# Token groups of 128 instead of 112 behind the attention of a two-layer image model

## The chip, the cores and the metric

The kernel runs on one core of a Trainium2 chip. The core has a matrix engine (TensorE, PE in the profile, with its weight loads as PEld), three engines for elementwise work (VectorE, DVE; ScalarE, ACT; GpSimd, POOL), a queue engine (SyncE, SP), an on-chip memory SBUF of 128 partitions, a small accumulator memory PSUM, and 16 DMA engines. The metric is the time of one execution on the device in microseconds (us). Before the change it is 1744.01 us, the median of 3 runs (1739.07 to 1748.02).

## The reference

The input x is a float32 image batch, 2 x 256 channels x 56 x 56. Two layers follow; a token is one pixel with its 256 channels, and there are N = 6272 of them.

```
x = x + proj_o(attention_7x7(LN_channels(x)))            # layer 0, 8 heads
t = tokens(x)
t = t + (LN_t(t) + sum over the 2 best of 8 experts: w_e * MLP_e(LN_t(t)))
x = image(t)
x = x + relu(o1 + bn(tri_conv(o1)))                       # layer 1
    with o1 = relu(bn(tri_conv(LN_channels(x))))
t = tokens(x)
t = t + sum over the 2 best of 8 experts: p_e * MLP_e(LN_t(t))
x = image(t)
```

The hidden size of an expert is 256 in layer 0 and 512 in layer 1. tri_conv is a 3 x 3 convolution with weights quantised to -1, 0, 1; bn takes its statistics over the whole batch.

## The kernel before

An image is cut into 7 strips of 8 rows, 14 strips in all, 448 tokens each (`NT`). A strip is cut into 4 groups (`NTT`) of 112 tokens (`TT`), each a block of 8 rows by 14 columns: a group is what stands on the partitions at one time. There are 56 groups (`NTOK`).

The attention has its own use for the block of 112 queries, which the change leaves alone: queries, keys, scores and weighted sums (L1441 to L1540) run per block, and the loop over blocks is a hand-written order on every engine. What comes behind it, once a strip is complete, is `leave` (L1545): the normalised result is copied into `oc` (DVE, L1589), per group four records of `pw` on PE (two channel halves, L1602) project it, and DVE adds the input `xr` (L1610). Then the strip is handed to the routing.

Both layers route alike. `norm` (L765) takes per group the mean and variance (`bn_stats`, L713, `bn_aggr`, L715, both DVE), scales (`u`, ACT, L735), transposes on PE (`pu`, L781) with a copy on ACT (`ut`, L786), and multiplies with the gate (`pl`, L795): per group two matmuls, four records, that stream 8 columns each. In layer 0 the sum of token and norm is stored in the DRAM buffer `x_mid`. `settle` (L809) takes the two best experts on DVE, and ranks the tokens of each expert by small matmuls with triangular and all-one matrices (`rk`, L854 to L857). From the ranks come row numbers `pos`, and POOL sends each group's rows by two indirect DMAs into the expert buffer `xs` (L891), in layer 1 with three small operations ahead of them (L887 to L889). A strip in layer 0 is settled with its neighbour, in layer 1 as the list `BATCHES` says.

The experts (`experts_in_order`) read `xs` in tiles of 256 rows: transposes `pt` (L1112), first product `ph` (L1144), second product `py` (L1163), and an indirect DMA that scatters the result to `ys` in token order (L1175). The first tiles of a layer can start when the first 10 (layer 0) or 9 (layer 1) strips are routed (`FIRST`); the rest of the rows is sent beside the running experts.

Between the layers, `combine` (L1786) runs per strip: it fetches the two results of each token (`got`, L1211), adds them with their weights (DVE, L1230, and ACT, L1222), normalises over the channels, transposes (`pu`, L1239), and two copies on ACT write the strip into the padded image `pad` (L1801). The first three strips are done before the first convolution, the others beside it, driven by the convolution's step counter. The convolution works by units of two strips and four components (order 1, 2, 0, 3): `component` (L1818 to L1820) forms differences `v` of rows of `pad` on POOL, and splits them in `hi` (ACT) and `lo` (DVE) for the matmuls `pc` (L1845). Component 3 of a unit reads one row beyond the unit, which is the first row of the next strip. The second convolution (L1988) works on the image alone. `residual` (L2118) adds it up in channel layout (DVE, L2127; ACT, `nr`, L2130), transposes back to tokens (`pt`, L2139), and adds `x_mid` (L2145); `all_strips` (L2167) interleaves residual, norm and settle of consecutive strips in an order written out by hand, and `fence` (L2156) waits for the early scatters on POOL before the experts of layer 1 start.

The last loop (L2268) fetches `got` (L2273, two groups a piece), adds with weights (DVE, L2278), transposes (L2287), copies into the strip's `o_out` (ACT, L2293), and stores a whole strip (L2298).

Of the kernel before, what the change touches and what calls it, by code (L numbers as in the profile page):

```python
# [11 lines left out]
F32 = mybir.dt.float32  # L12
# [9 lines left out]
P = 128  # L22
# [46 lines left out]
EARLY = tuple(max(0, (TOP * NT * n - E * (G - 1)) // G) for n in FIRST)  # L69
# [563 lines left out]
def metaformer(ctx: ExitStack, tc: tile.TileContext, a: dict, out: bass.AP, flag):  # L633
# [31 lines left out]
    ids = rt.tile([TT, NTOK], F32, tag="ids", name="ids")  # L665
# [4 lines left out]
    x_mid = dram.tile([len(STRIPS), TT, NTT, C], F32, tag="x_mid", name="x_mid", bufs=1)  # L670
# [7 lines left out]
    minus_half = const.tile([TT, NTT], F32, tag="minus_half", name="minus_half")  # L678
# [11 lines left out]
    order = const.tile([TT, E], F32, tag="order", name="order")  # L690
# [3 lines left out]
    before_f = const.tile([TT, TT], F32, tag="before_f", name="before_f")  # L694
    nc.sync.dma_start(before_f, a["before"])
    before_w = const.tile([TT, TT], BF16, tag="before_w", name="before_w")
    nc.vector.tensor_copy(before_w, before_f)
    all_w = const.tile([TT, P], BF16, tag="all_w", name="all_w")
# [3 lines left out]
    base_t = tabs[:TT, T_BASE : T_BASE + E]  # L702
# [5 lines left out]
    def token_stats(tp, src, eps, root):  # L708

        stats = tp.tile([TT, NTT, 6], F32, tag="t_stats", name="t_stats")  # L710
        mv = tp.tile([TT, NTT, 2], F32, tag="t_mv", name="t_mv", bufs=3)
        for t in range(NTT):
            nc.vector.bn_stats(stats[:, t, :], src[:, t, :])  # L713
        for t in range(NTT):
            nc.vector.bn_aggr(mv[:, t, :], stats[:, t, :])  # L715
        rstd = tp.tile([TT, NTT], F32, tag="t_rstd", name="t_rstd", bufs=3)
        nmr = tp.tile([TT, NTT], F32, tag="t_nmr", name="t_nmr", bufs=3)
        nc.vector.tensor_scalar_mul(nmr, mv[:, :, 0], -1.0)
        if root:
            nc.scalar.activation(rstd, mv[:, :, 1], AF.Sqrt, bias=eps[:TT])  # L720
        yield
        if root:
            nc.vector.reciprocal(rstd, rstd)
            nc.vector.tensor_tensor(nmr, nmr, rstd, ALU.mult)
        else:
            nc.gpsimd.tensor_tensor(rstd, mv[:, :, 1], eps[:TT].to_broadcast([TT, NTT]), ALU.add)
            nc.gpsimd.tensor_tensor(rstd, rstd, minus_half, ALU.pow)
            nc.gpsimd.tensor_tensor(nmr, nmr, rstd, ALU.mult)
            yield
            yield  # L730
        return rstd, nmr

    def scaled(dest, src, rstd, nmr):
        for t in range(NTT):
# [10 lines left out]
    def routing(layer, wp, tp, ps):  # L745
# [4 lines left out]
        if layer == 1:  # L750
            gate_b = wp.tile([TT, E], F32, tag="gate_b", name="gate_b")
            nc.sync.dma_start(gate_b, a[pre + "gate_b"].partition_broadcast(TT))
        lgs = wp.tile([TT, NTOK, E], F32, tag="lgs", name="lgs")
        most = wp.tile([TT, TOP, NTOK], F32, tag="most", name="most")
        pos = wp.tile([TT, TOP, NTOK], I32, tag="pos", name="pos")
        wgt = rt.tile([TT, TOP, NTOK], F32, tag="wgt", name="wgt", bufs=2)
        chosen = wp.tile([TT, NTOK], F32, tag="chosen", name="chosen")
        seen = wp.tile([TT, E], F32, tag="seen", name="seen")
        nc.vector.memset(seen, 0.0)
        seen_b4 = wp.tile([TT, E], BF16, tag="seen_b4", name="seen_b4")  # L760
# [4 lines left out]
        def norm(i, src, late=False):  # L765
# [4 lines left out]
            row = rows[i] = tp.tile([TT, NTT, RW], F32, tag="u", name="u", bufs=U_BUFS[layer])  # L770
            u = row[:, :, :C]
            if layer == 0 or i >= FIRST[1]:
                eng.memset(row[:, :, R_EX + 1 :], 0.0)
                eng.tensor_copy(row[:, :, R_ID], ids[:, i * NTT : (i + 1) * NTT])
            scaled(u, src, rstd, nmr)
            yield
            ut = tp.tile([P, KC, NT], F32, tag="ut", name="ut", bufs=1)
            for k in range(KC):
                pu = ps.tile([P, 512], F32, tag="aux", name="pu")
                for t in range(NTT):  # L780
                    nc.tensor.transpose(  # L781
                        pu[:, t * TT : (t + 1) * TT],
                        u[:, t, k * P : (k + 1) * P],
                        ident[:TT, :TT],
                    )
                nc.scalar.copy(ut[:, k, :], pu[:, :NT])  # L786
            if layer == 0:
                eng.tensor_tensor(src, src, u, ALU.add)
                nc.sync.dma_start(x_mid[i], src)
                yield  # L790
            lg = lgs[:, i * NTT : (i + 1) * NTT, :]
            pl = ps.tile([TT, NTT, E], F32, tag="pl" if layer else "aux", name="pl")
            for t in range(NTT):
                for k in range(KC):
                    nc.tensor.matmul(  # L795
                        pl[:, t, :],
                        ut[:, k, t * TT : (t + 1) * TT],
# [4 lines left out]
            if layer == 1:  # L802
                yield
                nc.vector.tensor_tensor(lg, pl, bcast(gate_b, 1, [TT, NTT, E]), ALU.add)
# [4 lines left out]
        def settle(strips):  # L809


            n = len(strips) * NTT
            t0 = strips[0] * NTT
            us = [rows.pop(i) for i in strips]
            full, row = [TT, n, E], (TT, n)

            def small(name, shape=(TT, n, E), dt=F32):
                return tp.tile(list(shape), dt, tag=f"{name}_{n}", name=name, bufs=1)
# [13 lines left out]
            hot = small("hot", (TT, TOP, n, E))  # L832
            at = [chosen[:, t0 : t0 + n], small("at", (TT, n))]
            rest = small("rest")
            first_max(lg, m[0], hot[:, 0], at[0])
            for q, u in enumerate(us if layer == 0 or strips[0] >= FIRST[1] else ()):
                small_eng.tensor_copy(u[:, :, R_EX], at[0][:, q * NTT : (q + 1) * NTT])
# [7 lines left out]
            seen_b = small("seen_b", (TT, E), BF16)  # L845
            nc.vector.tensor_copy(seen_b, seen)
            here = small("here", (TT, E))
# [5 lines left out]
            rk = ps.tile([TT, n, E], F32, tag="aux", name="rk")  # L853
            nc.tensor.matmul(rk, before_w, hots, start=True, stop=False)  # L854
            nc.tensor.matmul(rk, all_w[:, :TT], bcast(seen_b, 1, full), start=False, stop=n == 1)
            for t in range(n - 1):
                nc.tensor.matmul(  # L857
                    rk[:, t + 1 :, :],
                    all_w[:, :TT],
# [1555 lines left out]
```

## Time and profile before

| what | value |
|---|---|
| median of 3 runs | 1744.01 us (1739.07 to 1748.02) |
| profiled execution, own time | 1758.43 us |
| its span in the profile | 1756.6 us |
| mean granted TensorE clock | 0.901 |

The prediction shows the lines of the profile that it rests on. Two ways of reading recur. A line of a group of instructions names the source line, the engine, output <- input with their shapes, the count, busy time and the mean of one in ns, and the engine's idle time just before with what ended it. A line of a window gives start and end, length, then the busy microseconds and instruction count of each engine in that stretch, the granted clock, the share of time that the DMA engines were busy, and GB/s. A float32 matmul appears as two records. Matmuls are pipelined: where some stand in a row, the time of the row minus the last one, divided by the others, is the pitch at which they follow each other, and it is shorter than the duration of one.

Where the time lies, by the starts of the first instructions of each stage:

| stage | us of the span |
|---|---|
| attention, with routing of layer 0 beside it | 0 to 512 |
| experts of layer 0 | 512 to 808 |
| first strips back into the image | 808 to 840 |
| first convolution, other strips beside it | 840 to 1005 |
| second convolution | 1005 to 1150 |
| residual, norm and routing of layer 1 | 1150 to 1295 |
| experts of layer 1 | 1295 to 1690 |
| last additions and output | 1690 to 1756.6 |

### The profile page before, as it was taken

The page shows a single profiled execution, that of the slowest core. Times are in us where ns is not written, and L with a number is a line of the kernel's source. Part 1 is how long each engine was busy: PE and PEld are TensorE (multiplying, and loading weights), DVE is VectorE, ACT ScalarE, POOL GpSimd, SP SyncE. Part 2 cuts the span into 40 slices and gives each one's busy share as a digit, 9 for nine tenths or more (in the row PEclk, how much of TensorE's full clock was granted, in tenths as well). Part 3 has the DMA queues.
Part 4 walks back from the last instruction along what each step waited for, and adds up shares of the span by engine and source line. Part 5 has one row for each costly group of instructions (what it writes and reads, how often), then busy time and mean ns, then how long its engine had stood idle before and what let it go on. Part 6 is the DMA issues. An engine that isn't in the chain of part 4 may idle for free. (4 is left out here: it accounts for less than half of the span.)

```text
span 1756.6 us, 26034 instructions
## 1 busy us (share of the span) xinstructions
PE 1514.2 (86%) x8613; PEld 1185.1 (67%) x8613; DVE 973.3 (55%) x2697; ACT 700.4 (40%) x1386; POOL 672.9 (38%) x772
## 2 busy tenths in 40 slices
PE   5999998999868968994799969957689999999964
PEld 3555565555547757783688768746578888888842
DVE  4456676456645417794899888778733111111147
ACT  2544343353333324454454363235433334333322
POOL 2112345253343565453143323327835552222210
PEclk9999999899979989997899989955579999999975
DMA  7122324221166768795754000014467768888869
GB/s 237 43 65 87 107 86 124 70 81 60 55 192 195 246 220 320 255 336 160 198 151 123 3 0 1 11 47 128 134 215 266 266 228 303 286 278 294 287 182 306
DMA packets 93679, 291.78 MB, mean 166 GB/s; under 512 B 20711, under 2 KB 36027, under 8 KB 83776
## 3 DMA queue, kind: packets, MB, share of 16 engines
q1 hardware_dynamic: 68528, 231.79, 41.9%
q0 software_dynamic: 21200, 51.82, 8.2%
q10 hardware_dynamic: 3808, 6.42, 1.0%
q8 instruction: 70, 1.15, 0.3%
q14 instruction: 73, 0.60, 0.1%
HBM read 218.51 MB, written 74.20 MB: 167 GB/s over the span
## 5 line engine op out<-in xcount | busy, mean ns | idle before, releaser
L1144 PE MATMUL ph<-ut,w 128*128 128x256 f32 (+1 forms) x1472 | 311.5, 362 | 10.3 <-DMA w<-in_L_experts 5.3
L1173 DVE TENSOR_TENSOR y<-py,w 128x512 f32<-128x512 f32 (+1 forms) x120 | 76.8, 640 | 419.0 <-PE py L1163 349.6
L1163 PE MATMUL py<-w,h 128*128 128x256 f32 x1288 | 300.6, 382 | 3.5 <-DVE y L1173 1.5
L1144 PEld LDWEIGHTS ph<-ut,w 128*128 128x128 f32 x1472 | 251.6, 195 | 39.8 <-DMA w<-in_L_experts 6.0
L1163 PEld LDWEIGHTS py<-w,h 128*128 128x128 f32 x1288 | 245.0, 192 | 38.1 <-DVE y L1173 1.9
L891 POOL DMA_INDIRECT xs<-u,pos x224 | 218.3, 974 | 116.1 <-issue 52.8
L1175 POOL DMA_INDIRECT ys<-y,dest x136 | 137.4, 1010 | 242.0 <-DVE dest L1119 107.5
L1151 ACT ACTIVATE h<-ph,w 128x256 f32<-128x256 f32 (+1 forms) x368 | 162.6, 448 | 118.3 <-PE ph L1144 93.5
L1520 ACT ACTIVATE ex<-sc 112x476 f32<-112x476 f32 (+3 forms) x224 | 117.3, 573 | 178.2 <-PE sc L1510 162.5
L1116 ACT COPY ut<-pt 128x512 f32<-128x512 f32 (+1 forms) x120 | 65.1, 543 | 268.4 <-PE pt L1112 214.4
L1845 PE MATMUL pc<-lo,wq 128*128 128x448 f32 x336 | 131.5, 393 | 7.0 <-DVE lo L1820 6.9
L1845 PE MATMUL pc<-hi,wq 128*128 128x448 f32 x336 | 130.9, 392 | 3.4 <-DVE x L1869 3.2
L1540 DVE TENSOR_TENSOR acc<-av,acc 128x238 f32<-128x238 f32 (+3 forms) x224 | 87.5, 407 | 76.3 <-PE av L1530 65.6
L1530 PE MATMUL av<-ex,vals 112*64 112x238 f32 (+3 forms) x896 | 124.6, 399 | 5.8 <-DVE acc L1540 5.5
L1175 POOL DMA_INDIRECT ys<-y,to x81 | 81.8, 1009 | 119.7 <-DVE dest L1119 65.1
L1988 PE MATMUL pc<-hi,wq 128*128 128x448 f32 (+1 forms) x288 | 102.8, 366 | 17.9 <-ACT hi L1955 9.4
L1501 PE MATMUL sc<-q_im,keys 32*112 32x238 f32 (+3 forms) x896 | 98.6, 427 | 7.0 <-ACT ex L1520 6.8
L1988 PE MATMUL pc<-lo,wq 128*128 128x448 f32 (+1 forms) x288 | 101.8, 363 | 0.2 <-DVE lo L1956 0.2
L1818 POOL TENSOR_TENSOR v<-pad 128x928 f32<-128x928 f32 (+1 forms) x28 | 56.2, 2017 | 100.4 <-DVE lo L1820 49.5
L1530 PEld LDWEIGHTS av<-ex,vals 112*64 112x64 f32 x896 | 56.4, 141 | 55.8 <-issue 27.2
L1112 PE MATMUL pt<-ident,xg 128*128 128x128 f32 x434 | 71.2, 285 | 25.1 <-DMA xg<-xs 11.8
L1112 PEld LDWEIGHTS pt<-ident,xg 128*128 128x128 f32 x434 | 56.5, 148 | 39.8 <-ACT ut L1116 14.4
(279 smaller groups left out, 2532.3 us busy)
## 6 DMA issues: line engine op xcount, KB each, us to landing
w<-in_L_experts SPq DMA_DIRECT2D x64, 1154.0 KB
w<-in_L_experts SPq DMA_DIRECT2D x56, 641.0 KB
xg<-xs SPq DMA_DIRECT2D x97, 260.0 KB
acc<-in_fresh SPq DMA_DIRECT2D x14, 896.0 KB
got<-ys SPq DMA_DIRECT2D x14, 896.0 KB
got<-ys SPq DMA_DIRECT2D x28, 448.0 KB
xt<-in_x_tok SPq DMA_DIRECT2D x14, 448.0 KB
xr<-in_x_tok SPq DMA_DIRECT2D x14, 448.0 KB
```

What stands on the lines that cost most here:

```text
L891: w = nc.gpsimd.indirect_dma_start(xs[:, :], bass.IndirectOffsetOnAxis(ap=pos[:, j, t0 + t : t0 + t + 1], axis=0), us[t // NTT][:, t % NTT ...
L1112: nc.tensor.transpose(pt[:, k, i * P : (i + 1) * P], d["xg"][:, i, k * P : (k + 1) * P], ident)
L1144: nc.tensor.matmul(ph[:, :g], w1[:, k, f * P : (f + 1) * P], d["ut"][:, k, :g], start=k == 0, stop=k == KC - 1,)
L1151: nc.scalar.activation(d["h"][:, f, :g], ph[:, :g], AF.Gelu, bias=b1[:, f : f + 1])
L1163: nc.tensor.matmul(py[:, i, :], d["h"][:, f, i * P : (i + 1) * P], w2[:, f, :], start=f == 0, stop=f == NF - 1,)
L1175: o = nc.gpsimd.indirect_dma_start(ys[:, :], bass.IndirectOffsetOnAxis(ap=d["to"][:, i : i + 1], axis=0), y[:, i, :], None, bounds_check=T ...
L1501: nc.tensor.matmul(sc[h // 2][:, h % 2, :nq], keys[g][p, c, tx * TT : (tx + 1) * TT], q_im[p, c, r0:r1, c0:c1], start=True, stop=False,)
L1520: nc.scalar.activation(e[:, :, :nq], sc[j][:, :, :nq], AF.Exp, scale=HD**-0.5)
L1530: nc.tensor.matmul(av[VW * i : VW * (i + 1), :nq], vals[g % 3][:, tx, 2 * c + j, 2 * i : 2 * i + 2, :].rearrange("p a d -> p (a d)"), ex[j ...
L1540: added = nc.vector.tensor_tensor(d, av[:, :nq].rearrange("p (h w) -> p h w", w=c1 - c0), d, ALU.add)
L1845: nc.tensor.matmul(pc[:, :NT], wq[:, k, c, dx * C + o * P : dx * C + (o + 1) * P], part[:, :, k, dx : dx + W], start=m == 0, stop=m == 2 * ...
L1988: nc.tensor.matmul(pc[:, : 2 * ns * W], wq[:, k, c, dx * C + o * P : dx * C + (o + 1) * P], part[:, : 2 * ns, k, dx : dx + W], start=m == ...
```

## The change

Two neighbouring strips hold 896 tokens, seven groups of 128. Behind the attention the even strip of a pair now has three groups and the odd strip four; there are 49 groups (`NGR`). The block is 8 rows by 8 columns, two blocks a group. An even strip has seven blocks, so its last one is left over: it becomes half of the first group of the odd strip, together with the odd strip's own last block. A group can thus be made only of tokens that lie in two strips, and the buffers from which groups are read become rings of 512 columns, in which the even strip fills columns 64 to 511 and the odd strip 0 to 447.

```diff
+BW = 8
+NGR = N // P
+RING = NT + P // 2
+def groups_of(i):
+
+    at = 2 * NT // P * (i // 2) + NT // P * (i % 2)
+    return at, NT // P + i % 2
...
-    x_mid = dram.tile([len(STRIPS), TT, NTT, C], F32, tag="x_mid", name="x_mid", bufs=1)
+    x_mid = dram.tile([N, C], F32, tag="x_mid", name="x_mid", bufs=1)
...
-        for t in range(NTT):
+        for t in range(n):
             nc.vector.bn_stats(stats[:, t, :], src[:, t, :])
...
-            for t in range(NTT):
+            for t in range(ng):
                 for k in range(KC):
                     nc.tensor.matmul(
                         pl[:, t, :],
-                        ut[:, k, t * TT : (t + 1) * TT],
+                        ut[:, k, t * P : (t + 1) * P],
                         gate[:, k, :],
```

The image is written by runs of neighbouring blocks. An even strip writes one run of six blocks (48 of its 56 columns); an odd strip writes three: its own last block, the last block of the even strip, and its six others. So an even strip stands complete in the image only once the odd one has been written.

```diff
+    def runs_of(i, at=0, n=None):
+
+        ng = groups_of(i)[1]
+        runs = []
+        for t in range(at, ng if n is None else at + n):
+            col = (t - at) * P
+            if i % 2 and not t:
+                runs += [(col, i, NB - 1, 1), (col + P // 2, i - 1, NB - 1, 1)]
+                continue
+            x = 2 * (t - i % 2)
+            if runs and runs[-1][1] == i and runs[-1][2] + runs[-1][3] == x:
+                runs[-1] = (*runs[-1][:3], runs[-1][3] + 2)
+            else:
+                runs.append((col, i, x, 2))
+        return runs
+
+    def in_ring(i, t):
+
+        at = (P // 2 + t * P) if i % 2 == 0 else ((t - 1) * P if t else RING - P)
+        return slice(at, at + P)
...
-                pu = channels(strips_ps, "pu", xn)
-                for k in range(KC):
-                    nc.scalar.copy(
-                        blocks(inner(*STRIPS[i])[:, :, k]),
-                        pu[:, k].rearrange("p (t h w) -> p t h w", h=SR, w=TW),
-                    )
+                pu = strips_ps.tile([P, KC, 512], F32, tag="pu", name="pu", bufs=1)
+                channels(pu, xn)
+                for at, strip, x, m in runs_of(i):
+                    for k in range(KC):
+                        nc.scalar.copy(
+                            narrow(inner(*STRIPS[strip])[:, :, k])[:, x : x + m],
+                            in_blocks(pu[:, k, at : at + m * P // 2]),
+                        )
```

`leave` projects from the ring `oc`, `residual` transposes from the ring `nr`; both keep the rest of their form. The input for the first residual addition comes in the new order of tokens (`x_rows`), and `ids`, the target rows of the experts' results, follow it. The last loop again takes two groups a piece, so an even strip has pieces of two and one, an odd strip two and two; an even strip's output is stored after the first piece of the odd strip, and `o_out` has six buffers instead of five. The numbers of expert tiles and the early shares of them are the same before and after.

Counted over the kernel: `pw` from 112 matmuls to 98; `pl` from 224 to 196; `rk` with its all-one products from 117 to 103; transposes of groups (`pu` and the like) from 448 of 112 streamed columns to 392 of 128; `bn_stats` of groups behind the attention from 168 to 147; weighted additions on DVE from 216 to 190; scatters on POOL from 224 to 196; copies into the image from 28 to 56 and into the output from 56 to 84. Loads and stores move the same bytes in the same number of transfers.

## The prediction

> **What bounds the kernel now.** I read the share of each engine first, then the span in slices, then a table of windows by stage, and last the timeline and the waits inside the stages that the change touches. From the head of the page and its slices (one character is 43.9 us):
>
> ```profile
> PE 1514.2 (86%) x8613; PEld 1185.1 (67%) x8613; DVE 973.3 (55%) x2697; ACT 700.4 (40%) x1386; POOL 672.9 (38%) x772
> PE   5999998999868968994799969957689999999964
> DVE  4456676456645417794899888778733111111147
> PEclk9999999899979989997899989955579999999975
> DMA  7122324221166768795754000014467768888869
> ```
>
> TensorE leads over the whole, but the slices show stages with different limits: attention (0 to 512 us), the experts of layer 0 (to 808), a head in which no matmul of the convolutions can run yet (to 840), the first convolution (to 1005), the second (to 1150), residual and routing of layer 1 (to 1295, granted clock 0.5), the experts of layer 1 (to 1690), the tail (to 1756.6, clock 0.5). The windows (length, then busy time of PE, PEld, DVE, ACT, POOL, clock, DMA share, GB/s):
>
> ```profile
> 100.00:200.00 100.00, 96.31 (x705) 57.66 (x709) 63.03 (x182) 47.48 (x90) 20.69 (x25) 1.00 0.28 85
> 900.00:960.00 60.00, 59.27 (x299) 50.98 (x298) 60.00 (x142) 30.90 (x57) 24.65 (x15) 1.00 0.51 144
> 1220.00:1290.00 70.00, 47.09 (x270) 41.49 (x269) 52.04 (x212) 31.64 (x63) 52.95 (x108) 0.60 0.51 164
> 1710.00:1720.00 10.00, 4.30 (x18) 2.85 (x19) 7.27 (x18) 2.77 (x10) 0.00 (x0) 0.50 1.02 325
> ```
>
> In attention PE is the limit alone; in the first convolution PE and DVE are both full; in routing none is, so a loop of dependent steps sets the pace; in the tail the DMA engines are full.
>
> **Sizes.** 56 groups become 49 per layer, but 7 x 128 = 8 x 112. An operation that costs by the token columns that it streams saves nothing; one that costs per group saves an eighth. Bytes of every transfer stay.
>
> **Attention: -5 us (0 to -8).** Each group has four records of the output projection (pw, L1602): 28 go. A strip's 16 take 3.71 us, the last lasting 0.379, so the pitch is 0.222 and 28 x 0.222 = 6.2, of which two strips' share lies after 512 us. The gate logits (pl, L795) have four records a group: 16 take 1.74 us at full clock, pitch about 0.102. [...] The nearest row with 128 columns, the transposes of the expert rows (L1112, four in 0.60 us, the last 0.273), has a pitch of 0.109 where pu with 112 streamed columns has 0.103. So width costs about 6% instead of 14%: by the row 0.12 us a strip is won[...]. I take the row for pl and transposes: 11 x 0.12 = 1.3. With 5.3 for pw this is 6.6 of PE; PE stands idle 2 to 8 us in each 100 of this stage, so I count 5. DVE, ACT and POOL lose some 15 (7 residual adds at half size, stats, scaling, adds on POOL); PE covers all of it. The ring buffer adds no wait: strips finish in order, so the even strip's last block is there when the odd strip's first group needs it.
>
> **Experts of layer 0: -1.5 (0 to -4).** Rows, tiles and weights are the same; only the norms and scatters of the last strips beside them shrink. DMA share is 0.76.
>
> **Head: -1 (-2 to +1).** Strips 0 and 2 lose a group: one add pair (3.26 us per 8), one bn_stats (0.41), one scaling. Against that the odd strip's copies to the image go from 2 (0.49 each) to 6: two of 384 columns, four of 64. From 357 ns at 224 columns and 559 at 448 a copy is 0.155 plus 0.9 ns a column, an estimate: 2 x 0.50 + 4 x 0.21 = 1.84, +0.85 us, on the path once.
>
> **First convolution: -2 (-7 to +4).** DVE loses 12 additions of y x 0.647, 7 x 0.41 stats and 7 x 0.15 aggregates, 11.5 us with the head's. It is saturated, but so is PE, which waits only 10.3 us in this stage (6.9 for lo, 3.2 for x, 0.2 for hi), all that a faster DVE can give back; and PE's work (448 transposes of 112 columns for 392 of 128) stays. The change adds a wait: component (u,3) of the convolution reads the first row of strip 2u+2, whose last eight columns now come with strip 2u+3. It is rival three.
>
> **Second convolution, experts of layer 1: 0.** Neither has tokens in groups; the held scatters (20 to 18 groups of two) lie under a PE that is 98% busy.
>
> **Layer 1's residual and routing: -5.5 (-2 to -12).** Two chains end together at 1295.3. The first is the loop PE, DVE, PE, ACT:
>
> ```profile
> 1195.67 2.78 PE L795 MATMUL pl<-gate,ut 128*112 128x8 f32 x14 [0.42 <-ACT ut L786]
> 1198.31 1.94 PE L2139 MATMUL pt<-ident,nr 128*112 128x128 f32 x8
> 1201.46 0.27 PE L854 MATMUL rk<-hots,before_w 112*112 112x32 bf16 x1 [1.22 <-DVE hot L826]
> ...
> 1205.19 1.10 PE L795 MATMUL pl<-gate,ut 128*112 128x8 f32 x5 [0.42 <-issue]
> ```
>
> One strip takes 9.5 us from pl to pl. Of that pl is 3.2 (16 records at half clock, pitch 0.199), then choice and rank on DVE, rk, two halves of pu with a copy each. By the row a strip of 3.5 groups wins about 0.2 on pl, 0.1 on pu and pt, 0.1 on rk and its operands; half of DVE's 0.18 in stats and 0.15 in L2145 and of ACT's 0.26 in scaling are in the loop for some strips: 0.4 to 0.5 a strip, 12 to 13 strips, 5.5. [...] The other chain is POOL's scatters:
>
> ```profile
> L891 POOL DMA_INDIRECT xs<-u,pos x72 | 70.3, 977 | 26.2 <-issue 18.9 <-ACT ut L786 4.0 <-ACT nr L2130 1.7
> L888 POOL COPY u<-ids 112x1 f32<-112x1 f32 x36 | 10.4, 288 | 0.0
> ```
>
> 36 groups from 1175.86 to 1284.9 are 3.03 us each; the strips ahead of the ninth now have 31. A scatter of 128 rows takes 1.010 (ys, L1175) instead of 0.977, so 31 x 3.1 = 96 instead of 109: it ends 12 us earlier and the fence behind it (1288.49) with it. What is late next is the first chain, so 5.5, not 12. The planning on DVE between (1251.3 to 1256) stays.
>
> **Tail: -2 (0 to -6).** DVE's additions (L2278) go from 112 x 0.48 to 98: -6.7 us of DVE. But
>
> ```profile
> L2278 DVE SCALAR_TENSOR_TENSOR x<-got,wgt,x 112x256 f32<-112x256 f32 x112 | 46.2, 480 | 16.3 <-DMA got<-ys 15.8
> ```
>
> shows that DVE waits 15.8 us for data, the DMA share is 1.02 to 1.04 from 1700 to 1745, and the bytes are the same. [...] I take 2, from the last pieces (11 additions after the last landing, 4.5 us)[...]. 28 more output copies on ACT lie in its 70% idle time. An even strip's output goes out later, beside the odd one's: at the end at most 0.5 us.
>
> **Sum**: -5 -1.5 -1 -2 -5.5 -2 = -17 us. The profiled run took 1758.4 (span 1756.6 plus 1.8), so 1741.4, 0.99 of it; the median shown lies 0.8% lower, 1744.0, and the same share gives **1727 us**.
>
> **Rivals.** *First, everything that shrinks is a limit* (1709): routing falls with POOL's chain (-12), [...]convolution by DVE's 7, attention 7, experts and head 3: -35. For it: the full DVE and the two chains ending together. Against it: DMA full in the tail, PE's loop in routing. *Second[...]* (1738): [...]pl and transposes gain nothing, DVE's part is covered, the tail is DMA's. Only 3 us of pw, 2 of routing, 1 of head remain: -6, which is within 0.5%, about what a measurement can tell from no change (8.7 us). *Third, the wait on the odd strip* (1757): component (u,3) must have v (POOL 2.2 us), hi (0.97) and lo (1.11) after the last copy; with 1.84 of copies 6.4 us from the transposes. In before (1,3)'s v starts at 879.32 and strip 5's copies at 887.09, 7.8 later. In the instruction order of the changed kernel strip 5's transposes stand 29 matmuls x 0.215 = 6.2 us ahead of (1,3)'s first one, later units' 35 to 37; unit 0's only 10, but PE waits 6 us there now for lo of the next component. So about zero by order. What can break it is the queue in front: if the additions on the full DVE or the copies on ACT come late, each us beyond the slack is one of PE. At 2.8 us a unit, over six units, the other gains are gone; I price the case at 5 a unit, 30 - 17 = +13. That the grouping isn't applied is excluded by the order of instructions (pl 224 to 196 a kernel, scatters 224 to 196).
>
> **Numbers.** Forecast 0.56 (own range 1714 to 1735), first 0.20, second 0.13, third 0.11. Faster takes the first two and little else, 0.76; same 0.13; slower 0.11. Range 1705 to 1747: two tenths of doubt lie beyond, the third rival's full price and the extremes of the first.
>
> **What would show it.** pw at 196 records and a strip pitch in routing near 9.0; POOL's last early scatter about 12 us ahead of PE's last rank; the tail still near a DMA share of 1.0, some 2 us shorter; PE in the first convolution with no wait over 3 us at v of (u,3). It is wrong if PE waits there for lo at each unit, if the routing stage keeps its 145 us, or if the tail shrinks by 6.

## The result, and the profile after

The changed kernel takes 1718.76 us (median of 6 runs, 1716.31 to 1724.29), the kernel before 1743.89 (6 runs, 1737.36 to 1748.02). The ratio is 0.9864, with a 95% interval of 0.9838 to 0.9891: 1.4% faster. That is 24 us by the ratio and 25 between the medians, where 17 were forecast. The first profiled execution took 1717.5 us, of which 1715.7 are its span.

The head of the page of the changed kernel, with the slices of the span (42.9 us each):

```profile
PE 1494.3 (87%) x8445; PEld 1170.3 (68%) x8445; DVE 958.2 (56%) x2620; ACT 694.3 (40%) x1419; POOL 636.9 (37%) x729
PE   5999999899877979994989879957679999999964
DVE  3456667466645445976998888777743112111136
PEclk9999998899889989996999989955579999999975
DMA  7122324121267877984441000024457877888858
```

PE lost 20 us of busy time, DVE 15, POOL 36. None of these is the gain: it is a sum over stages, and one of them got slower. The first profiled execution of the kernel before took 1758.4, 14 us above its median, so both kernels were profiled once more, on one chip. Stage by stage, from the first instruction of one stage to that of the next; each of the two convolutions is counted to its last matmul, so that the first one is longer here than in the table of the time before:

| stage | before, first | before, second | after, first | after, second | second pair | forecast |
|---|---|---|---|---|---|---|
| attention | 516.2 | 513.9 | 496.4 | 491.7 | -22.2 | -5 |
| experts of layer 0 | 296.2 | 280.5 | 283.9 | 283.7 | +3.2 | -1.5 |
| head | 27.9 | 27.7 | 22.6 | 22.6 | -5.1 | -1 |
| first convolution | 171.1 | 169.9 | 179.0 | 179.4 | +9.5 | -2 |
| second convolution | 134.2 | 134.2 | 134.2 | 134.2 | 0 | 0 |
| residual and routing | 149.7 | 150.5 | 146.1 | 146.1 | -4.4 | -5.5 |
| experts of layer 1 | 396.3 | 396.8 | 394.7 | 395.4 | -1.4 | 0 |
| tail | 65.0 | 65.6 | 58.8 | 58.6 | -7.0 | -2 |

The head, the convolutions, routing and the tail repeat to within 1 or 2 us. Attention and the experts of layer 0 do not. Nine profiles of this document have the changed kernel's code in both stages: attention takes 491.7, 492.9 and 497.5 us in three of them on the chip of the second pair, 497.7 and 504.9 in two on another chip, and 491.7 to 504.9 in all. With the code of before it takes 513.9 to 516.5 in three profiles. So the gain in attention is well clear of this spread, 16 to 22 us on the chip of the second pair, but 7 us between two single profiles of this stage show nothing.

Windows of the changed kernel, as far behind the start of their stage as those of before in the prediction (start and end, length, busy time of PE, PEld, DVE, ACT, POOL, clock, DMA share, GB/s): attention, middle of the first convolution, routing, tail.

```profile
100.00:200.00 100.00, 99.75 (x722) 59.44 (x714) 63.59 (x187) 48.12 (x91) 22.66 (x28) 0.97 0.27 85
...
863.00:923.00 60.00, 53.24 (x240) 44.52 (x239) 59.04 (x123) 26.98 (x60) 22.07 (x14) 0.91 0.34 122
...
1190.00:1260.00 70.00, 43.40 (x225) 37.53 (x225) 48.73 (x207) 29.23 (x58) 39.87 (x82) 0.58 0.51 173
...
1675.00:1685.00 10.00, 5.31 (x21) 3.08 (x20) 7.79 (x19) 3.63 (x16) 0.00 (x0) 0.50 1.02 355
```

In attention PE has less idle time (0.25 us in this 100 instead of 3.7). In the convolution DVE is as full as before (59.04 of 60), but PE is not (53.24 instead of 59.27), and the granted clock is 0.91 instead of 1.00. In the tail the DMA share is what it was, 1.02.

The loop of the routing stage in the changed kernel (the timeline of PE):

```profile
1163.12 3.15 PE L822 MATMUL pl<-gate,ut 128*128 128x8 f32 x14 [0.45 <-ACT ut L813]
...
1172.45 2.30 PE L822 MATMUL pl<-gate,ut 128*128 128x8 f32 x10 [0.34 <-ACT ut L813]
...
1181.77 3.15 PE L822 MATMUL pl<-gate,ut 128*128 128x8 f32 x14 [0.45 <-ACT ut L813]
```

A strip takes 9.33 us from pl to pl, before 9.5, and an odd and an even one 18.65 together. The 14 records of pl (L822) take 3.15 us, before 2.78: with the last one left out (0.345 and 0.334) the pitch at half clock is (3.15 - 0.345) / 13 = 0.216 and (2.78 - 0.334) / 13 = 0.188. The quotient is 1.15; 128 to 112 is 1.14.

### The profile page after: what moved, and what is told of

Its sections match the earlier page's. It is cut to its first block, busy times and chain, and to the rows that moved or that the text cites. A ratio compares the mean times of both kernels' runs of the same rounds, so it can differ in the third digit from the quotient of the medians.

```text
span 1715.7 us, 25578 instructions
## 1 busy us (share of the span) xinstructions
PE 1494.3 (87%) x8445; PEld 1170.3 (68%) x8445; DVE 958.2 (56%) x2620; ACT 694.3 (40%) x1419; POOL 636.9 (37%) x729
## 5 line engine op out<-in xcount | busy, mean ns | idle before, releaser
L1182 PE MATMUL ph<-ut,w 128*128 128x256 f32 (+1 forms) x1472 | 307.7, 360 | 13.0 <-DMA w<-in_L_experts 11.0
L1182 PEld LDWEIGHTS ph<-ut,w 128*128 128x128 f32 x1472 | 250.0, 194 | 41.6 <-DMA w<-in_L_experts 12.9
L929 POOL DMA_INDIRECT xs<-u,pos x196 | 195.4, 997 | 114.7 <-issue 37.5
L1602 PEld LDWEIGHTS av<-ex,vals 112*64 112x64 f32 x896 | 56.1, 140 | 52.0 <-issue 27.9
L1573 PEld LDWEIGHTS sc<-q_im,keys 32*112 32x112 f32 x896 | 46.0, 175 | 49.7 <-ACT ex L1592 25.3
```

Source lines behind the costliest of these rows:

```text
L929: w = nc.gpsimd.indirect_dma_start(xs[:, :], bass.IndirectOffsetOnAxis(ap=pos[:, j, t0 + t : t0 + t + 1], axis=0), at_of[t][0][:, at_of[t] ...
L1182: nc.tensor.matmul(ph[:, :g], w1[:, k, f * P : (f + 1) * P], d["ut"][:, k, :g], start=k == 0, stop=k == KC - 1,)
L1573: nc.tensor.matmul(sc[h // 2][:, h % 2, :nq], keys[g][p, c, tx * TT : (tx + 1) * TT], q_im[p, c, r0:r1, c0:c1], start=True, stop=False,)
L1602: nc.tensor.matmul(av[VW * i : VW * (i + 1), :nq], vals[g % 3][:, tx, 2 * c + j, 2 * i : 2 * i + 2, :].rearrange("p a d -> p (a d)"), ex[j ...
```

## The experiments

Each kernel is the changed one with a small edit, where nothing else is said. All ratios are to the kernel before on the same chip.

**The kernel before, once more.**

> The kernel before, once more, for a second profile. The first profiled run of it took 1758.4 us, 14 more than its median, and against the changed kernel its attention stage was 19.8 us longer and its experts of layer 0 12.3 us longer. If these two gains are real, attention ends near 516 and the experts take near 296 again, about 1758 in all. If they are half chance of the granted clock, this run is near 1744 and the attention ends at 505 to 510.

1740.9 us, attention 513.9, experts of layer 0 280.5. So the gain in attention is real, and the one of the first pair in the experts of layer 0 (296.2 to 283.9) is not the change's.

**The changed kernel, once more.**

> The changed kernel, once more, for a second profile: near 1719 us. The stages without a clock throttle in them (second convolution 134, experts of layer 1 395, tail 58.8) should repeat within 1 us; the first convolution near 179 if its extra 8 us over before belong to the kernel, nearer 171 if they were chance of the clock.

1713.4 us. The second convolution, the experts of layer 1 and the tail repeat (the tail's granted clock is low, but a steady 0.50), and the first convolution takes 179.4: its extra 8 us belong to the kernel.

**Strips into the image one component earlier.** In the step counter of the first convolution:

```diff
-                i, late = divmod(n + 3 + COMPS, COMPS)
+                i, late = divmod(n + 4 + COMPS, COMPS)
```

> The changed kernel with each strip from the fifth on brought back into the image one component of the first convolution earlier. Theory one (component 3 of a unit now waits for the odd strip's copies, which come one step too late): the waits of POOL's row differences on the copies into the image shrink, and the first convolution goes from 179 to about 171, the whole to about 1711. Theory two (the extra 8 us are the clock or DVE alone): the stage stays within 2 us of 179 and the total at 1719.

The first convolution took 170.9 us, the other stages stayed (attention 492.9, routing 146.4, tail 60.1), and the total is 1709.08 us (ratio 0.9811, 0.9777 to 0.9844). The waits of POOL in the first convolution, in us, times and longest: first the kernel before, then the changed one, then the edited one.

```profile
POOL v L1818 <- DVE lo L1820: 49.5, 13, 4.8
POOL v L1818 <- ACT pad L1801: 47.3, 5, 29.1
```

```profile
POOL v L1896 <- ACT pad L1879: 61.0, 5, 24.2
POOL v L1896 <- DVE lo L1898: 44.1, 14, 4.6
```

```profile
POOL v L1896 <- DVE lo L1898: 75.8, 22, 6.1
POOL v L1896 <- ACT pad L1879: 24.0, 1, 24.0
```

Each of the first two kernels has one long wait for copies at the start. The other four last 6.7, 0.6, 5.4 and 5.5 us before the change and stand ahead of the first component of the next unit; in the changed kernel they last 10.9, 10.3, 6.1 and 9.4 and stand ahead of component 3, as the third rival of the prediction says. With the strips a component earlier POOL waits for copies at the start alone, and otherwise mostly for DVE to free a buffer, which means that it is ahead. Theory one holds for POOL. What PE waits for in the changed kernel is less simple:

```profile
PE pc L1923 <- DVE lo L1898: 5.5, 5, 2.4
PE pu L1278 <- ACT xn L762: 4.9, 3, 1.7
PE pc L1923 <- DVE x L1945: 1.9, 1, 1.9
```

Its waits for `lo` (5.5 us, before 6.9) are shorter than before. The new ones stand ahead of the transposes of the strips themselves (4.9 us, before none) and wait for their scaled rows `xn` from ACT. In the edited kernel these waits are 1.8 us.

**The same, two components earlier** (with n + 5, and strip 5 taken up with strips 3 and 4).

> The changed kernel with the strips brought back into the image two components of the first convolution earlier instead of one. If the copies' lateness is fully gone with one component (POOL's waits on them fell from 61 to 24 us, all in the first unit), the first convolution stays at 171, within 2, and the total at 1709; if some wait was left, 168 and 1706; if the transposes and additions now come too early and push the matmuls back, above 173.

First convolution 176.3, total 1715.72 (0.9831, 0.9804 to 0.9858). The waits for copies are gone as before (one of 30.2 us at the start is left), but 5 of the 8 us are back: the third of the cases named.

**The control: the kernel before, one component earlier.** The same edit in the kernel before.

> The kernel before with its strips one component earlier, as a control. Theory one (only the changed kernel's component 3 waits for a late strip): the first convolution stays at 170, within 2, and the total at 1742. Theory two (the earlier start is a gain of its own, whatever the groups): it falls by 5 to 8 as it did in the changed kernel.

First convolution 174.9, 5 us more than before; ratio 1.0018 (0.9999 to 1.0037). Here too POOL waits for copies only at the start (once, 28.9 us), and nothing is won by it. The earlier start of both kinds of strips is no gain of its own; it pays where component 3 has to wait for the odd strip.

**Only the odd strips earlier.**

```diff
-                i, late = divmod(n + 3 + COMPS, COMPS)
-                i = 2 * (i - 1) + 3 + late
-                if late < 2 and 5 <= i < len(STRIPS):
-                    coming.append(combine(i))
+                for late in range(2):
+                    i, r = divmod(n + 4 - late + COMPS, COMPS)
+                    i = 2 * (i - 1) + 3 + late
+                    if r == late and 5 <= i < len(STRIPS):
+                        coming.append(combine(i))
```

> The changed kernel with only the odd strips brought back into the image one component earlier, in the same step as the even strip before them; the even strips stay. Component 3 waits for odd strips alone, so if that wait is all, the first convolution falls to 171 as with both kinds moved, and the total to 1709. If the earlier even strips mattered too, or if two strips in one step pile up on DVE, 174 to 179.

163.9 us, better than either theory: 15 less than in the changed kernel's own profiles and 6 less than before the change. The total is 1725.12 us on a chip where the kernel before takes 1773.75: 0.9713 (0.9683 to 0.9744). The edit with double POOL operations below, in which this stage is as in the changed kernel, takes 177.4 in it and has 0.9805 (0.9777 to 0.9833) on the same chip. The window over the whole first convolution, first of the changed kernel, then of this one:

```profile
803.00:982.00 179.00, 166.07 (x750) 140.86 (x750) 164.68 (x306) 70.69 (x141) 60.75 (x29) 0.94 0.29 108
```

```profile
824.00:988.00 164.00, 158.65 (x749) 137.34 (x750) 154.18 (x306) 71.10 (x142) 57.52 (x29) 0.97 0.33 118
```

The instructions are the same in number. Of the 15 us, 7.6 are idle PE (12.9 to 5.3), and the rest is mostly busy time at half clock: summed over windows of 2 us, busy time times what is missing of the clock is 10.5 us in the changed kernel (6.8 to 10.9 over all profiles of this code), 4.3 here, 5.3 before.

The edit does more than its expectation says. The odd strip does not come in the same step as the even one before it: the strips are now evenly spaced, two components apart. Their transposes stand behind 6, 8, 10 and 12 components' matmuls, where the edit with both kinds earlier has them in pairs behind 8 and 9, 12 and 13. And the DVE's additions of the experts' results gain by the new places:

```profile
L1230 DVE SCALAR_TENSOR_TENSOR x<-got,wgt,x 112x256 f32<-112x256 f32 x88 | 51.2, 647 | 4.7 <-DMA got<-ys 4.7
```

```profile
L1265 DVE SCALAR_TENSOR_TENSOR x<-got,wgt,x 128x256 f32<-128x256 f32 x78 | 56.1, 758 | 0.0
```

```profile
L1265 DVE SCALAR_TENSOR_TENSOR x<-got,wgt,x 128x256 f32<-128x256 f32 x78 | 39.4, 553 | 0.0
```

These are the additions in the first convolution before, in the changed kernel and here. The change took ten of them away, and yet they take 5 us more. An addition beside which POOL does nothing takes 0.47 us in all three kernels. Each that takes over 0.6 us runs beside a `v` of POOL (11 before, 16 in the changed kernel, 6 here) and lasts up to 2.5 us:

```profile
868.10 4.83 POOL L1896 TENSOR_TENSOR v<-pad 128x928 f32<-128x928 f32 x3 [10.32 <-ACT pad L1879]
868.40 4.81 DVE L1265 SCALAR_TENSOR_TENSOR x<-got,wgt,x 128x256 f32<-128x256 f32 x3
```

Here, in the changed kernel, three additions start with three pieces of `v` that waited 10 us for copies, and take as long as these. The time beyond 0.47 us an addition sums to 15 us before, 22 in the changed kernel and 6 here. How the 15 us are shared between the end of the wait, the even spacing and the shorter additions is not shown: no run changes one of them alone.

**Odd strips earlier, and strips 3 and 4 with them; and the changed kernel beside it.**

```diff
-                if n < 2:
+                for _ in range((3, 0)[n] if n < 2 else 0):
                     push_all()
```

> The version with the odd strips one component earlier (first convolution 163.9, PE idle 5.2 us in it), and in the first unit strips 3 and 4 also one component earlier, so that component 3 of unit 0 finds its copies. If the 24 us wait of POOL on copies in the first unit is what is left, the first convolution falls to 160 to 162; if DVE, full in the first 40 us, can't do the additions earlier, it stays at 164 or gets longer. In either case about 15 us below the changed kernel run beside it.

> The changed kernel unaltered, timed on the same chip as the next run, so that its distance to the version with earlier odd strips is measured on one chip. First convolution 177 to 179, ratio to before 0.980 to 0.987.

On their chip (the kernel before: 1786.18) the changed kernel takes 1741.88 us (0.9764, 0.9709 to 0.9819; first convolution 179.3), the edit 1735.06 (0.9723, 0.9667 to 0.9779; first convolution 168.9). The 15 us below the changed kernel that were expected are 10. It is better than the change alone, but 5 us worse in the stage than with the odd strips only, so the first unit is best left as it is; 4 us of its gain went into the routing stage (151.9, beside 147.9), for a reason that was not followed up. The change itself is worth more on this chip than on that of the result: the two intervals do not overlap. No profile of the kernel before was taken here, so where it wins more is open.

**The tail with loads to 112 partitions.**

```diff
-                nc.sync.dma_start(y, rows[:, t0 : t0 + m])
+                nc.sync.dma_start(
+                    y112[:TT],
+                    flat[piece * TT * PT * TOP : (piece + 1) * TT * PT * TOP, :].rearrange(
+                        "(p t j) c -> p t j c", t=PT, j=TOP
+                    ),
+                )
+                piece += 1
```

> The changed kernel, but the last loop loads its experts' results as the kernel before did, 28 loads to 112 partitions of 4 KB each (the same bytes in all); the additions run on 112 of the 128 partitions, so the last additions of 16 partitions are left out. Number and shape of the rest stay. Theory one[...]: the tail goes from 58.8 back to about 65, the total up by 6, and the rate from 329 to about 294 GB/s. Theory two (the gain came from the 14 fewer additions on DVE and from earlier output): the tail stays at 59 to 60.

The tail takes 67.2 us and the total is 1725.82 (0.9905, 0.9875 to 0.9936): the whole gain of the stage is gone, and a little more. The DMA view of the tail gives packets, bytes and the mean rate (bytes over the length of the view); in order: before, changed, loads to 112 partitions.

```profile
DMA packets 7420, 19.39 MB, mean 294 GB/s; under 512 B 688, under 2 KB 4272, under 8 KB 7409
```

```profile
DMA packets 7852, 19.39 MB, mean 329 GB/s; under 512 B 672, under 2 KB 4256, under 8 KB 7840
```

```profile
DMA packets 7403, 19.38 MB, mean 287 GB/s; under 512 B 672, under 2 KB 4256, under 8 KB 7392
```

Each has 28 loads: 448 KB in the first and the last, in the changed kernel 21 of 512 KB and 7 of 256. A window of each in which loads run and no store yet, in the same order:

```profile
1698.00:1703.00 5.00, 2.15 (x9) 1.15 (x8) 4.07 (x11) 1.72 (x6) 0.00 (x0) 0.50 1.04 256
```

```profile
1663.50:1668.50 5.00, 2.65 (x11) 1.26 (x9) 4.61 (x12) 2.13 (x11) 0.00 (x0) 0.50 1.01 372
```

```profile
1662.00:1667.00 5.00, 2.29 (x9) 1.08 (x8) 3.57 (x9) 1.88 (x10) 0.00 (x0) 0.50 1.03 251
```

The number of additions on DVE is 98 in the last two alike, 112 in the first. So the additions were worth nothing while the loads set the pace; the way of loading, to 128 partitions instead of 112, is all of it.

**The projection's records put back.**

```diff
-                for i in range(m):
-                    at = in_ring(g, t + i)
+                for i in range(2):
+                    at = in_ring(g, min(t + i, n - 1))
```

> The changed kernel with the 28 records of the output projection put back (in each even strip the third group is projected a second time, into a part of PSUM that nobody reads). Attention took 515 us in two profiles of the kernel before and 494 in three of the changed one; of the 20, 7 is matmul work at full clock, 5 is idle PE and 5 is half clock. Theory one (the records cost their own time only): attention 494 to 500, total +6. Theory two (work in front of the strip's chain brings back idle time and half clock as well): attention to 505 or more, total +12.

Attention 508.8 us, the experts of layer 0 279.7, the total 1724.01 (0.9876, 0.9841 to 0.9911). Three other kernels of this list ran on the same chip; their attention, experts of layer 0, and both together: the kernel before with the earlier strips 516.5, 277.6, 794.1; this one 508.8, 279.7, 788.5; two components earlier 497.0, 284.8, 781.8; with the vector work put back 497.1, 283.3, 780.4. In these profiles 28 records of 0.222, 6 us, bring back 12 in attention, as theory two says; but two kernels with the same code there differ by 7 on one chip, and the profiled execution of this one took 3 us more than its median. Four of the twelve are given back in the next stage, and by the medians of the totals the records cost 7 to 8 us (1724.01, against 1715.72 with the strips two components earlier and 1716.67 with the vector work put back). So the records are worth 7 to 8 of the 13 that the change wins in both stages, little more than their pitch, and theory two is not shown. The sum over the stretch from the first strip's projection to the twelfth's (windows of 2 us; work at full clock is what remains of the length without idle PE and without what the half clock costs):

| kernel | length | idle PE | cost of half clock | work at full clock |
|---|---|---|---|---|
| before, two profiles | 387.8, 385.2 | 25.6, 17.7 | 20.7, 28.7 | 341.5, 338.8 |
| changed, two profiles | 370.6, 366.7 | 17.2, 15.7 | 20.4, 17.5 | 333.0, 333.5 |
| records put back | 383.8 | 14.4 | 32.6 | 336.8 |
| its chip: two components earlier; vector work put back | 371.8, 372.1 | 13.6, 17.2 | 26.3, 22.8 | 331.9, 332.1 |
| another chip: odd strips earlier; POOL's operations twice | 371.3, 379.9 | 14.0, 15.5 | 23.2, 31.8 | 334.2, 332.6 |

The work fell by 7 us with the change, and with the records it is 5 above the two kernels on the same chip. The rest of what came back with them is time at half clock, 6 to 10 us; the last row, in which both kernels have the same code in this stretch, shows that this differs by 9 between two profiles without any cause in the code.

**The vector work put back.** One more bn_stats, bn_aggr and scaling in the norm of each even strip in attention.

```diff
+        again = range(1 if n == 3 and not root else 0)
+        for t in again:
+            nc.vector.bn_stats(stats[:, t, :], src[:, t, :])
...
+            if layer == 0 and not late and ng == 3:
+                scaled(u[:, :1], src[:, :1], rstd[:, :1], nmr[:, :1])
```

> The changed kernel with one more bn_stats, bn_aggr and scaling in the norm of the even strips in attention, as many per pair of strips as the kernel before had (about 1.2 us on DVE and ACT per pair, nothing on PE). Theory one (DVE and ACT are covered by PE in attention): attention stays at 494, within 3. Theory two (the chain from the projection through the norm sets the idle time of PE): attention rises by 4 or more.

Attention 497.1, total 1716.67 (0.9843, 0.981 to 0.9876). Theory one: PE covers it.

**POOL's small operations twice.**

```diff
                         nc.gpsimd.tensor_copy(u[:, R_EX : R_EX + 1], at[0][:, t : t + 1])
+                        nc.gpsimd.memset(u[:, R_EX + 1 :], 0.0)
+                        nc.gpsimd.tensor_copy(u[:, R_ID : R_ID + 1], ids[:, t0 + t : t0 + t + 1])
+                        nc.gpsimd.tensor_copy(u[:, R_EX : R_EX + 1], at[0][:, t : t + 1])
```

> The changed kernel with the three small POOL operations of each of the 31 early groups of layer 1 done twice (about 0.5 us a group, some 15 us on POOL in the routing stage, more than the 12 that the change took off). Theory one (the loop of PE, DVE and ACT sets the stage, POOL only ends beside it): the routing stage stays at 146, within 2 to 4 us, since POOL's scatters now end 15 us ahead of the first expert tile. Theory two (POOL's chain sets it): 158 or more.

The routing stage takes 146.3 us (changed: 146.1); total 1741.64, ratio 0.9805 (0.9777 to 0.9833). The fence that follows the last early scatter, in the view of its tile (duration, start): the changed kernel first, then this one.

```profile
L2236 POOL DMA_DIRECT2D some<-xs x1: 611/611/611, 1247.4 to 1247.4; - x1
```

```profile
L2238 POOL DMA_DIRECT2D some<-xs x1: 613/613/613, 1280.5 to 1280.5; - x1
```

The first expert tile starts at 1262.1 and 1288.6, so the fence moved from 14.7 us ahead of it to 8.1, near the 6.8 of the kernel before. That is less than the 15 us that were expected of the edit, but nearly all that the change had won there, and the stage didn't notice. POOL's own saving there was worth nothing.

## Why the prediction was right, and where it was not

The total was forecast 8 us too high (1727 us), and that it came so near is in part luck: it is a sum of terms that were wrong in both directions. Attention, head and tail gave 26 us more than the sum counted on the pair of one chip, the first convolution took 11.5 and the experts of layer 0 some 5 back. Of the six stages that were given a range only routing ended in it.

**Attention (-5, measured -16 to -22): the mechanism was right, the term was mis-sized.** The sum counted PE's removed work, 6.6 us, and the decomposition shows 7 (341.5 and 338.8 to 333.0 and 333.5). The step that failed is the discount on it: "PE stands idle 2 to 8 us in each 100 of this stage, so I count 5". PE's idle time and half-clock time were treated as fixed, so that removed work could only be lost in them. In the two pairs of profiles they fell as well, idle time by 5 us and the cost of half clock by 6 on the mean. The second is not certain, since this cost runs from 17.5 to 31.8 us over the profiles of the changed code. The 28 records of pw are worth 7 to 8 us; some 5 of the 13 us that attention and the following stage win together on that chip have no experiment behind them. A part of them can be read in the traces: PE's waits for `oc` ahead of the projection's records are 5.3 to 7.5 us in the three profiles of the code before and 2.1 to 4.2 in seven of the changed code, and 3.8 with the records put back; why `oc` comes earlier is not shown. That DVE and ACT are covered by PE was right (497.1 with their work put back).

**Experts of layer 0 (-1.5, measured +3.2).** Three us of attention's gain are given back here. With the records put back attention was 12 longer and this stage 4 shorter in single profiles, so the two are better taken in one sum: -19 on the pair of one chip, -13 on another, where -6.5 was forecast.

**Head (-1, measured -5.1): mis-sized.** The term took one add pair, one bn_stats and one scaling against copies estimated at 1.84 us. The six copies of an odd strip took 1.40 us. The first additions started 4.4 us after the first load instead of 5.9: the first strip brings three groups, a seventh less in bytes than before, and they go to 128 partitions. The two were not told apart. The rest, from the first addition to the first matmul of the convolution, went from 22.0 to 18.2: a chain in which nearly every step shrank (additions on ACT and POOL, scaling, statistics for strips of three groups), not the one add pair of the sum.

**First convolution (-2, measured +9.5): wrong, and the third rival had the right wait, but not the way in which it costs.** The step that failed is "So about zero by order". It counted 29 to 37 matmuls between the odd strip's transposes and component 3's first one, at 0.215 us, against 6.4 us of copies, v, hi and lo, and took POOL, ACT and DVE as free when their turn comes, though DVE was full (60.00 us of 60 in the prediction's window). POOL's waits on copies behind the first one rose from 18 us over 4 to 37 over 4. PE's work at full clock in the stage is 155.5 us in the first profiles of both kernels. Its idle time was 10.3 and 8.2 us in the two profiles before and is 12.9 and 12.8 in the two after; the cost of half clock was 5.3 and 6.1 and is 10.5 and 10.9. These two are the 7.9 and 9.5 us that the stage lost in the two pairs. In the units 1 to 4, where POOL waits for copies, PE does not pause at component 3 itself, which is where the prediction looked ("no wait over 3 us at v of (u,3)" held): it pauses at the components that follow and at the transposes of later strips. The price of 5 us a unit was too high: 9.5 over six units is 1.6.

Moving the strips in the changed kernel takes the loss away, and the same edit in the kernel before costs 5 us; so the loss comes from the places of the strips in the order, which the change made too late. That POOL's wait alone is the cause is not shown, for the same edits shorten DVE's additions; shorter additions alone are not enough either, since the edit in the kernel before shortens them too (0.58 us in the mean instead of 0.65) and the stage gets longer. The other term, "DVE loses 12 additions of y x 0.647", was wrong too: 0.647 us is a mean over 77 additions of 0.47 and 11 of 1.9 that ran beside `v`. In the changed kernel ten fewer additions take 5 us more, because 16 meet a `v`. So DVE's saved work was not won; with the odd strips earlier it was, and more, and the 163.9 us are 6 below the kernel before. Whether the kernel before would gain as much from evenly spaced strips was not tried.

**Routing (-5.5, measured -4.4): right, by other terms than written.** The working took the row of L1112 for pl and transposes, 6% for 128 columns. That does not hold for pl: with 128 columns of `ut` instead of 112 its pitch rose by 15%, from 0.188 to 0.216; 196 records at the second are 42.3 us, 224 at the first 42.1, nothing won. At a granted clock of 1.00, in attention, 16 records take 1.95 us where they took 1.74. Transposes won little (L2221 and L810 together 52.4 us, before 54.8). The second rival, in which pl and transposes gain nothing, leaves 2 us for this stage; the measured 3.6 and 4.4 of the two pairs lie above it. What the rest is was not tried; what is left in the loop is the statistics, residual addition and scaling of the three-group strips. That POOL's chain is not what is late was right, and shown (146.3 us with its small operations twice, beside 146.1).

**Tail (-2, measured -7.0): the wrong side of the weighing.** The step that failed took "the DMA share is 1.02 to 1.04 from 1700 to 1745" for a full rate. While loads run alone the share is 1.04 at 256 GB/s to 112 partitions and 1.01 at 372 to 128: it tells that packets are under way, not how fast they move. The prediction's own sign of being wrong, a tail shorter by 6, came true. With all other work of the loop in place the stage takes 67.2 us with loads to 112 partitions and 58.7 with loads to 128. The loads alone became faster by almost a half (256 to 372 GB/s); over the whole stage, in which stores run beside them, it is an eighth of the time. That loads to 128 partitions are the faster ones here is shown; by what they are is not, and no trace of the kernel before told it ahead of the result.

**Rivals.** The first (-35) rightly took the tail for a stage that shrinks (7.0 us measured) and had its mechanism wrong in routing; the second (-6) was right that pl gains next to nothing (all its records 64.4 us busy before, 63.8 after); the third was at work inside the gain, through POOL's and DVE's delay rather than PE's wait at component 3.

## What to carry to other kernels

Here a group of 128 in place of 112 saved next to no PE time where tokens are the columns (all records of pl 64.4 us busy before, 63.8 after). It saved the fixed work per group (the 28 records of pw are worth 7 to 8 us), and it loaded faster into SBUF (372 GB/s to 128 partitions, 251 and 256 to 112), which decided the tail, where loads set the pace, though the busy share of the DMA engines stood at 1.01 to 1.04 in all three. When a regrouping lets a buffer be completed by a later producer, find each consumer that used the earlier one, and try the later producer one step earlier: here this was worth 13 to 15 us of the stage, more than half of what the change itself won, with the producers evenly spaced by the same edit. A mean time of an instruction can hide two kinds (0.647 us was 77 additions of 0.47 and 11 of 1.9): look at what runs beside the long ones before a saved instruction is counted at the mean. And in a stage that PE fills, price an added wait of PE with the half clock that may come with it (in the first convolution 2.6 and 4.6 us more of idle PE came with 5.2 and 4.8 us more of half clock in the two pairs), and do not read a few us from one profile.

## What the runs showed that was not expected

In dense stretches of attention the granted clock fell, to 0.57 in the mean of 4 us, without a pause of PE. Windows of the second profile of the changed kernel:

```profile
125.00:135.00 10.00, 10.00 (x96) 6.07 (x88) 4.07 (x12) 7.28 (x14) 1.82 (x1) 1.00 0.36 90
135.00:139.00 4.00, 4.00 (x15) 1.83 (x13) 3.16 (x7) 1.17 (x2) 0.00 (x0) 0.57 0.38 115
139.00:169.00 30.00, 30.00 (x224) 18.91 (x225) 17.16 (x49) 14.93 (x28) 7.56 (x8) 1.00 0.23 72
169.00:173.00 4.00, 4.00 (x20) 1.75 (x21) 3.69 (x14) 1.17 (x2) 0.36 (x2) 0.57 0.71 203
```

PE is busy throughout in these windows, and in four microseconds out of 34 the granted clock is 0.57. 34 us is also the length of a strip, so whether time or the kind of work sets it was not told apart. In other profiles of the same code some of these dips are missing.

At the change from the first image to the second, PE pauses (2.9 us of 300 to 306 in the second profile of the changed kernel) and then runs at a lower clock for a time that differs between profiles: windows of the second profile of the changed kernel, of the kernel before, and of the kernel with loads to 112 partitions, which has the changed code in this stage; all three ran on one chip.

```profile
306.00:317.00 11.00, 11.00 (x57) 6.45 (x54) 5.61 (x16) 6.03 (x12) 3.86 (x4) 0.69 0.33 115
```

```profile
312.00:333.00 21.00, 18.29 (x76) 10.53 (x75) 8.79 (x28) 9.86 (x19) 6.71 (x9) 0.59 0.22 66
```

```profile
304.00:322.00 18.00, 17.00 (x69) 10.26 (x70) 6.91 (x23) 8.73 (x18) 3.94 (x4) 0.53 0.21 71
```

The windows are 11, 21 and 18 us long, at 0.69, 0.59 and 0.53. So the shorter time of the first is not the change's; it is part of the 22 us by which the second pair differs in attention.

The other surprise is how much the order of two strips is worth: the best kernel of the study is the changed one with the odd strips one component earlier. It stands at 0.9713 of the kernel before, on a chip where the change without this edit (with POOL's small operations doubled) stands at 0.9805.
